# TensorE tile shapes in a two-layer graph attention kernel: transposes as quarter products with the identity, scores in sixteen 32x32 tiles

## The chip, the cores and the metric

The kernel runs on one core of a Trainium2 chip. The metric is the device time of one execution in microseconds (us); three runs of the kernel before gave 3501.76, 3508.07 and 3508.48, so a median of 3508.07. One execution more was recorded by the hardware profiler, and every duration below comes from that one.

## The reference

For each of 16 graphs x is 1024 nodes by 256 features, and adj says which pairs of nodes are joined. Two layers follow each other; all numbers are float32.

```python
# layer 0: multi-head attention without projections, then an MLP
h = maximum(layernorm(x), 0)
normed = layernorm(h) * gamma1 + beta1          # 8 heads of 32 features: queries = keys = values
scores = einsum('bhqd,bhkd->bhqk', qkv, qkv) / sqrt(32)
attn = softmax(where(adj > 0, scores, -inf))
h = h + einsum('bhqk,bhkd->bhqd', attn, qkv)
y = layernorm(h) * gamma2 + beta2
x = x + h + gelu(y @ W1 + b1) @ W2 + b2
# layer 1: one head of graph attention, 256 wide
f = maximum(layernorm(x), 0);  u = f @ W
logits = (u @ a_1).T + u @ a_2 + (u @ a_12) @ u.T
att = softmax(where(adj > 0, leaky_relu(logits, 0.2), -9e15))
x = x + elu(f @ W_1 + (att @ f) @ W_2)
```

## The kernel before, in words

**Tiles and stages.** `fast_path` holds the whole program; `general_path` is a fallback that a flag would start. Per graph, `attention` (line 931) walks 32 units: 2 halves of 512 queries, 2 groups of 4 heads, 8 blocks of 128 keys; 512 units in all. A unit has two steps on TensorE. `scores` (line 935, product on line 950) multiplies, for each of four heads j, a 32x128 piece of keys with a 32x512 piece of queries. The transposed features `kT` have head j on partitions 32j to 32j+31, so each product sits on 32 rows of the array and all 128 columns; the result fills 128 partitions of a PSUM bank of its own (`s`). VectorE adds the mask (line 971), ScalarE takes the exponential (line 974). `weigh` (line 982, product on line 987) runs one unit later: the weights, 128 keys by 512 queries, are multiplied with 128x32 values of each head, on all 128 rows and 32 columns of the array (`o`). After 8 key blocks `total` (line 896) sums the weights with ones, 128x32 again (`den`), and `finish` (line 914) transposes sums and outputs (`ptds`, `ptos`), divides, and adds to `h`. The sums come out 32 times over, and only every 32nd column of the transposed sums is read.

Between the units lies the rest of the previous graph, in pieces: `expand` and `contract` (the MLP, `ph` and `po`), `project`, `values`, `weights`, `attend` (layer 1: `puT`, `pg`, `lg`, `pf`, `pa`). All their products go through the helper `matmul` (line 565), which cuts the 128 stationary columns in four quarters of 32, so that they have the shape of `o`, 128 rows by 32 columns:

```python
    quarters = [True]

    def matmul(out, lhsT, rhs, start=True, stop=True):
        if not quarters[0]:
            nc.tensor.matmul(out, lhsT, rhs, start=start, stop=stop)
            return
        for c in range(0, P, HD):
            nc.tensor.matmul(out[c : c + HD], lhsT[:, c : c + HD], rhs, start=start, stop=stop)
```

When the attention of the last graph is over, `close_attention` (line 1042) sets the flag to False, and what is left of the last graph is multiplied without quarters.

**Transposes.** Blocks of 128x128 are transposed with TensorE's transpose against the identity, on the whole array: two `ptk` groups per half of a graph (`turn` in `prologue`, line 796, product on line 801), `pty` (`turn` in `rest`, line 1107, line 1117), `ptf` (`turn1`, line 1187, line 1193), four blocks each and four groups of each kind per graph; and in `finish` `ptds` and `ptos` (line 922), four blocks each, four times per graph; once in `setup` (line 672).

**Order.** Six generators (`stream_a` for the units, `stream_b` for the rest, `stream_p`, `stream_c`, `stream_m`, `stream_s`) each name a place in time, and the one with the lowest place goes on; every engine then keeps the order in which its instructions were written. Transposes wait in a list, `turns`, which `make_turns` (line 885) empties just before the scores of a unit. Waits between engines are semaphores put in from the tiles' uses. PSUM: two score tiles of two banks each, one bank for `o`, three for all else.

Of the kernel before, what the change touches and what calls it, by code (L numbers as in the profile page):

```python
# [9 lines left out]
F32 = mybir.dt.float32  # L10
# [6 lines left out]
P = 128  # L17
# [476 lines left out]
def fast_path(  # L494
# [28 lines left out]
    nc = tc.nc  # L523
# [34 lines left out]
    def ps_tile(shape, name, dtype=F32):  # L558
        return psm.tile(shape, dtype, tag="ps", name=name)
# [5 lines left out]
    def matmul(out, lhsT, rhs, start=True, stop=True):  # L565
# [3 lines left out]
        for c in range(0, P, HD):  # L569
            nc.tensor.matmul(out[c : c + HD], lhsT[:, c : c + HD], rhs, start=start, stop=stop)  # L570

# [21 lines left out]

    ident = const.tile([P, P], F32, name="ident")
    make_identity(nc, ident)
    ident8 = const.tile([P, P], FP8, name="ident8")
    nc.vector.tensor_copy(ident8, ident, saturate=False)  # L600
    ones = const.tile([P, HD], F32, name="ones")
# [58 lines left out]
    def setup():  # L660
        wl, wa, wT, wb = (lp1.tile([P, DC, D], F32, tag="e1", name=f"stage_{i}") for i in range(4))
        weights_to_load.extend([(wl, W), (wa, a_12)])
        for t, src in rows_to_load:
            nc.sync.dma_start(t, src)
        for t, src in weights_to_load:
            nc.scalar.dma_start(t, src.rearrange("(c p) n -> p c n", p=P))
        yield

        for oc in range(DC):
            pt = ps_tile([P, DC, P], f"p_wT_{oc}")  # L670
            for ic in range(DC):
                nc.tensor.transpose(pt[:, ic, :], wl[:, ic, oc * P : (oc + 1) * P], ident)
            nc.scalar.copy(wT[:, oc, :], pt.rearrange("p c q -> p (c q)"))
        clock[0] += 0.5
        yield

        def product(dst, lhs, rhs, n, name):

            for oc in range(DC):
                pp = ps_tile([P, n], f"p_{name}_{oc}")  # L680
                for kc in range(DC):
                    matmul(
                        pp,
                        lhs[:, kc, oc * P : (oc + 1) * P],
                        rhs[:, kc, :n],
                        start=(kc == 0),
                        stop=(kc == DC - 1),
                    )
                nc.scalar.copy(dst[:, oc, :], pp)

        product(wb, wa, wT, D, "wb")
        clock[0] += 1.7
        yield
        product(wm, wT, wb, D, "wm")
        product(w_a2.unsqueeze(2), wT, a2c.unsqueeze(2), 1, "w_a2")
        product(wo2[:, :, D : D + 1], wT, a1c.unsqueeze(2), 1, "w_a1")
        nc.gpsimd.memset(wo2[:, :, D + 1 : D + 2], 0.0)
        clock[0] += 2.0
        yield


        sq = lp1.tile([P, DC * D], F32, tag="e1", name="sq")
        few = smallp.tile([P, 2 * DC], F32, tag="few", bufs=1, name="few")
        wmf = wm.rearrange("p c n -> p (c n)")
        nc.vector.tensor_tensor(sq, wmf, wmf, op=ALU.mult)
        nc.vector.tensor_tensor(few[:, :DC], w_a2, w_a2, op=ALU.mult)
        nc.vector.tensor_tensor(few[:, DC:], wo2[:, :, D], wo2[:, :, D], op=ALU.mult)
        nc.vector.tensor_reduce(seen[:, 0:1], sq, axis=mybir.AxisListType.X, op=ALU.add)
        nc.vector.tensor_reduce(seen[:, 1:2], few, axis=mybir.AxisListType.X, op=ALU.add)
        yield  # L710
# [42 lines left out]
    def prologue(b, st):  # L753
# [42 lines left out]
        def turn(i):  # L796
            clock[0] += 0.5
            pt = ps_tile([P, NG, CW], f"ptk_{b}_{i}")
            for g in range(NG):
                for j in range(TPC):  # L800
                    nc.tensor.transpose(  # L801
                        pt[:, g, j * P : (j + 1) * P], va[:, i * TPC + j, g * P : (g + 1) * P], ident
                    )
            nc.scalar.copy(kT[:, :, i * CW : (i + 1) * CW], pt)

        steps = [
# [107 lines left out]
    def finish(b, qh, g, ds, os):  # L914
        h = hs[b]
        finished[b, qh] = finished.get((b, qh), 0) + 1
        clock[0] += 1.0
        pts = []
        for n, c in (("ds", ds), ("os", os)):
            pt = ps_tile([P, TPH, P], f"pt{n}_{b}_{g}_{qh}")  # L920
            for t in range(TPH):
                nc.tensor.transpose(pt[:, t, :], c[:, t * P : (t + 1) * P], ident)  # L922
            pts.append(pt.rearrange("p t (j d) -> p t j d", d=HD))
        rl = smallp.tile([P, TPH, GH], F32, tag="rl", name=f"rl_{b}_{g}_{qh}")
        nc.vector.reciprocal(rl, pts[0][:, :, :, 0])
        ot = tmpp.tile([P, TPH, GH, HD], F32, tag="w2", bufs=3, name=f"ot_{b}_{g}_{qh}")
        nc.vector.tensor_mul(ot, pts[1], rl.unsqueeze(3).to_broadcast([P, TPH, GH, HD]))
        ho = h[qh][:, :, g * P : (g + 1) * P]
        nc.gpsimd.tensor_add(ho, ho, ot.rearrange("p t j d -> p t (j d)"))

    def attention(b, st):
# [3 lines left out]
        def scores(qh, g, kt):  # L935
            qs = slice(qh * QW, (qh + 1) * QW)
            sc = [
                psc.tile([P, 2, QW], F32, tag=f"sc{i}", name=f"s_{b}_{g}_{qh}_{kt}_{i}") for i in range(2)
            ]

            by_pe = 2 if b == 0 else 0
            if by_pe:
                for j in range(by_pe):
                    matmul(
                        sc[j // 2][:, j % 2, :], ident8, st[qh][:, kt // 2, :, kt % 2], start=True, stop=False
                    )
                clock[0] += 0.45
            for j in range(GH):
                r = slice(j * HD, (j + 1) * HD)
                nc.tensor.matmul(  # L950
                    sc[j // 2][:, j % 2, :],
                    kT[r, g, kt * P : (kt + 1) * P],
                    kT[r, g, qs],
                    start=j >= by_pe,
                    stop=True,
                )
            mb = st[qh][:, kt // 2, :, kt % 2].unsqueeze(1).to_broadcast([P, 2, QW])
            es = []
            if b == 0 and kt % 2:

                odd = midp.tile([P, 2, 2, QW], F32, tag="mid", name=f"odd_{g}_{qh}_{kt}")
            for i in range(2):
                if b == 0 and kt % 2:
                    e = odd[:, i]
                elif kt == 0:
                    e = accp.tile([P, 2, QW], F32, tag=f"acc{i}", name=f"acc_{b}_{g}_{qh}_{i}")
                else:
                    e = ep.tile([P, 2, QW], F32, tag="e", name=f"e_{b}_{g}_{qh}_{kt}_{i}")
                masked = sc[i]
                if 2 * i >= by_pe:  # L970
                    nc.vector.tensor_tensor(e, masked, mb, op=ALU.add)  # L971
                    masked = e
                es.append(e)
                weights = lambda e=e, masked=masked: nc.scalar.activation(e, masked, AF.Exp, scale=SCALE)  # L974
                if i == 0:
                    weights()
            return es, weights
# [96 lines left out]
    def rest(b, st, tails):  # L1074
# [32 lines left out]
        def turn(c):  # L1107
            if st["y", c][1] is not None:
                run_deferred(st["y", c][1])
            y = st["y", c][0]  # L1110
            for i in range(TPC):
                defer(4.0 * i + 2.0, lambda t=c * TPC + i: add_residuals(t))
            yT[c] = tmpp.tile([P, DC, CW], F32, tag="yT", name=f"yT_{b}_{c}")
            pt = ps_tile([P, DC, CW], f"pty_{b}_{c}")
            for dc in range(DC):
                for i in range(TPC):
                    nc.tensor.transpose(  # L1117
                        pt[:, dc, i * P : (i + 1) * P], y[:, i, dc * P : (dc + 1) * P], ident
                    )
            for dc in range(DC):  # L1120
                nc.vector.tensor_scalar(
                    yT[c][:, dc, :],
                    pt[:, dc, :],
                    g2[:, dc : dc + 1],
                    be2[:, dc : dc + 1],
                    op0=ALU.mult,
                    op1=ALU.add,
                )
# [58 lines left out]
        def turn1(c):  # L1187
            run_deferred(ready1[c])
            fT = st["fT"]
            pt = ps_tile([P, DC, CW], f"ptf_{b}_{c}")  # L1190
            for i in range(TPC):
                for dc in range(DC):
                    nc.tensor.transpose(  # L1193
                        pt[:, dc, i * P : (i + 1) * P], ft[c][:, i, dc * P : (dc + 1) * P], ident
                    )
            nc.scalar.activation(fT[:, :, c * CW : (c + 1) * CW], pt, AF.Relu)

        def project(qh, oc, fT, uT):
# [343 lines left out]
```

## Time and profile before

| what | before |
|---|---|
| median of three runs | 3508.07 us (3501.76 to 3508.48) |
| the profiled execution | 3501.46 us |
| its span, first to last instruction | 3499.6 us, so 1.9 us lie around it |
| TensorE busy / VectorE / ScalarE / GpSimd | 98% / 79% / 53% / 40% |
| matmul records on TensorE | 46590, and as many weight loads |
| granted TensorE clock, mean | 0.998 |
| instruction fetch | 6.03 MB, 0.7% of the DMA engines' time |

A float32 product appears as two matmul records, each with a weight load of its own; a transpose as one. Four quarters of one product are four records that run side by side and start 6 to 7 ns apart; "a pass" below is one such set. A record lasts longer than the distance to the next pass[...]; so the cost of a block of instructions is read from the start of its first record to the start of the next block, and not from busy time. In the timeline view the columns are the start in us from the span's start, the length from the first start to the last end, the engine, the line, the operation, the tiles written and read, the part of the array used (rows*columns), the operand and the number of records. The releasers named in brackets are inferred by the profiler from semaphores.

### The profile page before, as it was taken

How to read it: one execution, taken by the hardware profiler on the slowest of the kernel's cores; microseconds unless marked ns; L12 is line 12 of the kernel's file. 1: busy time of each engine (PE TensorE's matmuls, PEld its weight loads, DVE VectorE, ACT ScalarE, POOL GpSimd, SP SyncE). 2: the span in 40 equal slices, each digit the busy share in tenths (PEclk: the TensorE clock that was granted, in tenths of full speed). 3: DMA queues.
4: the chain of work that ended last, by engine and by line, in shares of the span. 5: the costliest groups of instructions: out<-in, count | busy, mean ns of one | idle time of the engine just before them, and what ended most of it. 6: DMA issues, size and time to landing. Idle time of an engine off the chain costs nothing.

```text
span 3499.6 us, 107320 instructions
## 1 busy us (share of the span) xinstructions
PE 3445.0 (98%) x46590; PEld 1673.9 (48%) x46590; DVE 2758.3 (79%) x5193; ACT 1857.8 (53%) x2184; POOL 1412.8 (40%) x1708
## 2 busy tenths in 40 slices
PE   6999999999999999999999999999999999999998
PEld 2244444444444444444444444444444444444477
DVE  6878788787877878888787888878878777887754
ACT  4555555555555555555555555555555555555522
POOL 3444443434434344343444534344344443434220
PEclk9999999999999999999999999999999999999999
DMA  7798889999899998989989899998989989899720
GB/s 183 147 182 173 181 164 185 182 186 188 161 187 176 191 184 165 181 167 190 195 167 183 165 185 185 177 190 164 186 177 191 183 165 179 171 191 182 147 63 14
DMA packets 281860, 597.81 MB, mean 171 GB/s; under 512 B 94882, under 2 KB 130084, under 8 KB 281380
## 3 DMA queue, kind: packets, MB, share of 16 engines
q0 software_dynamic: 124416, 453.04, 70.1%
q1 hardware_dynamic: 154276, 134.41, 15.5%
q8 instruction: 368, 6.03, 0.7%
q10 hardware_dynamic: 2688, 3.41, 0.3%
q14 instruction: 112, 0.92, 0.1%
HBM read 104.21 MB, written 16.78 MB: 35 GB/s over the span
## 4 chain that ended last, share of the span: by engine, by line
PE 94%; DVE 3%; DMA 1%; issue 1%; ACT 0%; POOL 0%; ACTq 0%; SPq 0%; DVEq 0%; POOLq 0%
PE s L950 15%; PE o L987 13%; PE pa L570 12%; PE po L570 12%; PE ph L570 12%; PE lg L570 10%; PE pg L570 3%; PE pf L570 3%; PE puT L570 3%; PE den L901 2%; PE ptf L1193 1%; PE pty L1117 1%; PE ptk L801 1%; PE ptos L922 1%; PE pa L567 1%
## 5 line engine op out<-in xcount | busy, mean ns | idle before, releaser
L974 ACT ACTIVATE e<-e 128x1024 f32<-128x1024 f32 x852 | 896.0, 1057 | 964.3 <-DVE e L971 728.3
L1011 POOL DMA_DIRECT2D acc<-e x864 | 754.9, 890 | 1438.3 <-DMA acc<-e 637.3
L971 DVE TENSOR_TENSOR e<-s,mk 128x1024 f32<-128x1024 f32 x852 | 1002.6, 1217 | 181.2 <-PE s L950 155.4
L950 PE MATMUL s<-kT 32*128 32x512 f32 x4096 | 592.5, 643 | 3.5 <-DVE odd L971 2.7
L987 PE MATMUL o<-e,va 128*32 128x512 f32 x3456 | 461.8, 605 | 2.1 <-ACT e L974 2.1
L570 PE MATMUL pa<-gw,e 128*32 128x258 f32 x7648 | 453.0, 380 | 0.0
L570 PE MATMUL lg<-fT,uT 128*32 128x256 f32 x7680 | 447.3, 379 | 0.0
L570 PE MATMUL ph<-yT,w 128*32 128x256 f32 x7808 | 446.5, 379 | 0.0
L570 PE MATMUL po<-w,hid 128*32 128x256 f32 x7680 | 439.3, 379 | 0.0
L570 PEld LDWEIGHTS ph<-yT,w 128*32 128x32 f32 x7808 | 255.3, 110 | 211.8 <-issue 51.1
L570 PEld LDWEIGHTS po<-w,hid 128*32 128x32 f32 x7680 | 250.3, 110 | 208.8 <-issue 58.3
L570 PEld LDWEIGHTS pa<-gw,e 128*32 128x32 f32 x7648 | 248.4, 110 | 212.0 <-issue 56.5
L570 PEld LDWEIGHTS lg<-fT,uT 128*32 128x32 f32 x7680 | 249.6, 110 | 209.0 <-issue 43.4
L1241 DVE SCALAR_TENSOR_TENSOR e<-lg,gw,mk 128x256 f32<-128x256 f32 x512 | 223.2, 477 | 72.0 <-PE lg L570 61.5
L1247 ACT ACTIVATE e<-e,shift 128x512 f32<-128x512 f32 x256 | 183.1, 717 | 181.6 <-DVE e L1246 116.0
L1144 DVE TENSOR_TENSOR hid<-ph,b1c 128x512 f32<-128x512 f32 x256 | 175.8, 687 | 91.6 <-PE ph L570 80.1
L950 PEld LDWEIGHTS s<-kT 32*128 32x128 f32 x4096 | 162.7, 184 | 163.8 <-issue 112.0
L987 PEld LDWEIGHTS o<-e,va 128*32 128x32 f32 x3456 | 68.6, 108 | 330.3 <-issue 187.3
L974 ACT ACTIVATE acc<-acc 128x1024 f32<-128x1024 f32 x124 | 131.1, 1057 | 132.9 <-DVE acc L971 128.4
L1246 DVE SCALAR_TENSOR_TENSOR e<-e 128x512 f32<-128x512 f32 x256 | 193.1, 754 | 8.8
L971 DVE TENSOR_TENSOR acc<-s,mk 128x1024 f32<-128x1024 f32 x124 | 146.1, 1218 | 20.2 <-PE s L950 19.8
L793 POOL TENSOR_TENSOR nrm<-nrm,g 128x256 f32<-128x256 f32 x128 | 112.9, 882 | 63.8 <-DVE nrm L727 63.8
(145 smaller groups left out, 3820.9 us busy)
## 6 DMA issues: line engine op xcount, KB each, us to landing
acc<-e POOLq DMA_DIRECT2D x864, 512.0 KB, 6.1
adj<-in_adj_dram SPq DMA_DIRECT2D x248, 256.0 KB, 5.6
h<-in_x_dram SPq DMA_DIRECT2D x64, 256.0 KB, 6.1
xb<-in_x_dram SPq DMA_DIRECT2D x128, 128.0 KB, 4.3
out_dram<-z SPq DMA_DIRECT2D x128, 128.0 KB, 4.0
adj<-in_adj_dram SPq DMA_DIRECT2D x4, 512.0 KB, 6.8
mk<-mq SPq DMA_TRANSPOSE x128, 6.5
w<-in_L_gnn_W_dram ACTq DMA_DIRECT2D x2, 1024.0 KB
```

Of the source, the lines that this page charges most:

```text
L570: nc.tensor.matmul(out[c : c + HD], lhsT[:, c : c + HD], rhs, start=start, stop=stop)
L793: nc.gpsimd.tensor_mul(nrm, nrm, g1)
L901: nc.tensor.matmul(den[j * HD : (j + 1) * HD, :], ones, acc[j // 2][:, j % 2, :], start=acc is accs[0], stop=acc is accs[-1],)
L950: nc.tensor.matmul(sc[j // 2][:, j % 2, :], kT[r, g, kt * P : (kt + 1) * P], kT[r, g, qs], start=j >= by_pe, stop=True,)
L971: nc.vector.tensor_tensor(e, masked, mb, op=ALU.add)
L974: weights = lambda e=e, masked=masked: nc.scalar.activation(e, masked, AF.Exp, scale=SCALE)
L987: nc.tensor.matmul(o[j * HD : (j + 1) * HD, :], va[:, kt, (g * GH + j) * HD : (g * GH + j + 1) * HD], es[j // 2][:, j % 2, :], start=(kt = ...
L1011: nc.gpsimd.dma_start(sums[g, qh][i], e, accum_op=ALU.add)
L1144: nc.vector.tensor_tensor(hid[:, f0 : f0 + 2, :], ph, b1c[:, f0 : f0 + 2].unsqueeze(2).to_broadcast([P, 2, CW]), op=ALU.add,)
L1241: nc.vector.scalar_tensor_tensor(e[:, j, :], lg[:, j, :], gw[:, kt, D : D + 1], st[c // 2][:, kt // 2, qs, kt % 2], op0=ALU.add, op1=ALU.add,)
L1246: nc.vector.scalar_tensor_tensor(e, e, ALPHA, e, op0=ALU.mult, op1=ALU.max)
L1247: ready = defer(2.5, lambda: nc.scalar.activation(e, e, AF.Exp, bias=shift))
```

## The change

Every TensorE instruction of the main part gets stationary tiles of 32 columns. Transposes become plain products with the identity as the moving operand, in four quarters (while the flag is True). The transposed sums keep only the one column of each head that is read: the moving operand is then `each_head`, 128x4, every 32nd column of the identity. Each head's score product is cut in four along the keys, so that the sixteen products of a unit lie on 32x32 tiles of the array. The order of the blocks on each engine stays as it was; VectorE gets one small copy at the start.

```diff
+    def transpose(out, src, columns=None):
+
+        if not quarters[0]:
+            nc.tensor.transpose(out, src, ident)
+            return
+        for c in range(0, P, HD):
+            nc.tensor.matmul(
+                out[c : c + HD], src[:, c : c + HD], ident if columns is None else columns, start=True, stop=True
+            )
...
+    each_head = const.tile([P, GH], F32, name="each_head")
+    nc.vector.tensor_copy(each_head, ident[:, ::HD])
...
-                    nc.tensor.transpose(
-                        pt[:, g, j * P : (j + 1) * P], va[:, i * TPC + j, g * P : (g + 1) * P], ident
-                    )
+                    transpose(pt[:, g, j * P : (j + 1) * P], va[:, i * TPC + j, g * P : (g + 1) * P])
...
-        for n, c in (("ds", ds), ("os", os)):
-            pt = ps_tile([P, TPH, P], f"pt{n}_{b}_{g}_{qh}")
+        for n, c, rhs in (("ds", ds, each_head), ("os", os, ident)):
+            pt = ps_tile([P, TPH, rhs.shape[1]], f"pt{n}_{b}_{g}_{qh}")
             for t in range(TPH):
-                nc.tensor.transpose(pt[:, t, :], c[:, t * P : (t + 1) * P], ident)
-            pts.append(pt.rearrange("p t (j d) -> p t j d", d=HD))
+                transpose(pt[:, t, :], c[:, t * P : (t + 1) * P], rhs)
+            pts.append(pt)
...
-        nc.vector.reciprocal(rl, pts[0][:, :, :, 0])
+        nc.vector.reciprocal(rl, pts[0])
...
-                nc.tensor.matmul(
-                    sc[j // 2][:, j % 2, :],
-                    kT[r, g, kt * P : (kt + 1) * P],
-                    kT[r, g, qs],
-                    start=j >= by_pe,
-                    stop=True,
-                )
+                for c in range(0, P, HD):
+                    nc.tensor.matmul(
+                        sc[j // 2][c : c + HD, j % 2, :],
+                        kT[r, g, kt * P + c : kt * P + c + HD],
+                        kT[r, g, qs],
+                        start=j >= by_pe,
+                        stop=True,
+                    )
```

The transposes of `setup`, of `pty` and of `ptf` call the new helper in the same way.

More of the change, by code (lines that the diff above doesn't have):

```diff
@@ L671, in setup @@
             for ic in range(DC):
-                nc.tensor.transpose(pt[:, ic, :], wl[:, ic, oc * P : (oc + 1) * P], ident)
+                transpose(pt[:, ic, :], wl[:, ic, oc * P : (oc + 1) * P])
             nc.scalar.copy(wT[:, oc, :], pt.rearrange("p c q -> p (c q)"))
@@ L918, in finish @@
         pts = []
-        for n, c in (("ds", ds), ("os", os)):
-            pt = ps_tile([P, TPH, P], f"pt{n}_{b}_{g}_{qh}")
+        for n, c, rhs in (("ds", ds, each_head), ("os", os, ident)):
+            pt = ps_tile([P, TPH, rhs.shape[1]], f"pt{n}_{b}_{g}_{qh}")
             for t in range(TPH):
-                nc.tensor.transpose(pt[:, t, :], c[:, t * P : (t + 1) * P], ident)
-            pts.append(pt.rearrange("p t (j d) -> p t j d", d=HD))
+                transpose(pt[:, t, :], c[:, t * P : (t + 1) * P], rhs)
+            pts.append(pt)
         rl = smallp.tile([P, TPH, GH], F32, tag="rl", name=f"rl_{b}_{g}_{qh}")
-        nc.vector.reciprocal(rl, pts[0][:, :, :, 0])
+        nc.vector.reciprocal(rl, pts[0])
         ot = tmpp.tile([P, TPH, GH, HD], F32, tag="w2", bufs=3, name=f"ot_{b}_{g}_{qh}")
-        nc.vector.tensor_mul(ot, pts[1], rl.unsqueeze(3).to_broadcast([P, TPH, GH, HD]))
+        os_t = pts[1].rearrange("p t (j d) -> p t j d", d=HD)
+        nc.vector.tensor_mul(ot, os_t, rl.unsqueeze(3).to_broadcast([P, TPH, GH, HD]))
         ho = h[qh][:, :, g * P : (g + 1) * P]
@@ L1116, in turn @@
                 for i in range(TPC):
-                    nc.tensor.transpose(
-                        pt[:, dc, i * P : (i + 1) * P], y[:, i, dc * P : (dc + 1) * P], ident
-                    )
+                    transpose(pt[:, dc, i * P : (i + 1) * P], y[:, i, dc * P : (dc + 1) * P])
             for dc in range(DC):
@@ L1192, in turn1 @@
                 for dc in range(DC):
-                    nc.tensor.transpose(
-                        pt[:, dc, i * P : (i + 1) * P], ft[c][:, i, dc * P : (dc + 1) * P], ident
-                    )
+                    transpose(pt[:, dc, i * P : (i + 1) * P], ft[c][:, i, dc * P : (dc + 1) * P])
             nc.scalar.activation(fT[:, :, c * CW : (c + 1) * CW], pt, AF.Relu)
```

## The prediction

> **What bounds the kernel now.** First the page: which engine fills the span, and what the chain that ended last is made of.
>
> ```profile
> PE 3445.0 (98%) x46590; PEld 1673.9 (48%) x46590; DVE 2758.3 (79%) x5193; ACT 1857.8 (53%) x2184; POOL 1412.8 (40%) x1708
> ...
> PE 94%; DVE 3%; DMA 1%; issue 1%; ACT 0%; POOL 0%; ACTq 0%; SPq 0%; DVEq 0%; POOLq 0%
> ```
>
> Then TensorE's waits, to see whether that engine is held up by anything.
>
> ```profile
> PE ptk L801 <- POOL va L794: 22.2, 4, 19.3
> PE s L570 <- ACT acc L974: 8.1, 2, 5.5
> PE ptos L922 <- DVE e L1241: 3.4, 14, 0.2
> ```
>
> The largest three of twelve lines add to 33.7 us, all twelve to about 45 of 3499.6, most of it in the first graph. From there to the last graph TensorE never stands still, so only the length of its own stream counts. That is read from the timeline, start to start; first a stretch in the middle.
>
> ```profile
> 1696.95 1.91 PE L570 MATMUL ph<-yT,w 128*32 128x256 f32 x32
> 1698.68 1.91 PE L570 MATMUL po<-w,hid 128*32 128x256 f32 x32
> 1700.52 0.66 PE L1117 MATMUL pty<-ident,y 128*128 128x128 f32 x4
> 1701.11 1.14 PE L950 MATMUL s<-kT 32*128 32x512 f32 x8
> 1702.18 1.06 PE L987 MATMUL o<-acc,va 128*32 128x512 f32 x8
> 1703.06 3.64 PE L570 MATMUL po<-w,hid 128*32 128x256 f32 x64
> 1706.62 1.14 PE L950 MATMUL s<-kT 32*128 32x512 f32 x8
> 1707.70 1.06 PE L987 MATMUL o<-e,va 128*32 128x512 f32 x8
> 1708.58 1.04 PE L901 MATMUL den<-acc,ones 128*32 128x512 f32 x8
> 1709.44 1.91 PE L570 MATMUL po<-w,hid 128*32 128x256 f32 x32
> ```
>
> ph to po, the same shape on both sides: 1.73 us for 8 passes of 256 columns, 0.216 a pass. po to pty: the same 8 passes take 1.84, so 0.11 more at the change to 128*128. The 64 records of po, 16 passes, are worth 3.46, and the scores come 3.56 later: again 0.11. den, between equal shapes, takes 0.86 for two passes of 512 columns, 0.43 a pass. The scores take 1.07 for the same two passes, o 0.88. The records' own starts split this. After a change the next record starts 90 to 96 ns after the last one has streamed: an emptying of the array. A score's first record lasts 692 ns and its second 587, so 105 ns are the first load of weights that nothing covers; for o after the scores it is 617 against 592, 25 ns.
>
> The last graph, where nothing is cut in quarters, gives the counter-proof; after it the smallest products of the start.
>
> ```profile
> 3379.80 2.75 PE L567 MATMUL ph<-yT,w 128*128 128x256 f32 x12
> 3382.39 0.60 PE L1117 MATMUL pty<-ident,y 128*128 128x128 f32 x4
> 3382.83 1.46 PE L567 MATMUL po<-w,hid 128*128 128x256 f32 x6
> ...
> 73.00 0.43 PE L570 MATMUL p_w_a<-a1c,stage 128*32 128x1 f32 x32
> 73.36 0.66 PE L922 MATMUL ptds<-ident,ds 128*128 128x128 f32 x4
> ```
>
> Between products on the whole array four transposes take 0.44 us, 0.109 each, with no gap on either side (12 passes of ph are worth 2.59, and pty comes after 2.59). So it is the shape that costs, not transposing. In the middle the same four take 0.59: 0.44, 0.055 for a first load, and 0.093 to empty the array before the scores. That last change, 128*128 to 32*128, alters the rows alone, and still empties the array; the trace has 236 of it.
>
> [...] The trace has 6.7 ns between float32 tiles; I use that.
>
> **Transposes ahead of the scores.** A transpose is one record of 0.109; the product with the identity is a float32 product, two passes, and a pass of 128 columns is half of the 0.216: again 0.109. So four blocks cost 8 x 0.109 = 0.872 in place of 0.44. Saved are the change in front (0.113) and the first load (0.055); a change to the scores remains. Before, with both changes: 0.113 + 0.586 = 0.699. After: 0.872 + 0.113 = 0.985. That is +0.286 for each of 176 such groups (60 pty, 60 ptf, 56 ptk, counted in the trace): +50.3 us. Eight groups in the first graph and the setup are followed by 128*32; there the change behind goes too, and it is +0.15: +1.2. All of it is on TensorE and thus on the path. The last graph's six keep the old form: 0.
>
> **Transposes of sums and outputs.** Before: 0.113 + 1.022 for the pair. After, ptds has 4 moving columns: the nearest row is p_w_a with one column, 32 records whose starts span 0.26 us (0.43 less 0.17 for the last one), so 0.033 for a pass of four. 8 passes: 0.26. ptos as above 0.872, then the change 0.113: together 1.245, so +0.11 for 60 pairs: +6.6 us. Four more pairs lie elsewhere, about 0. From below ptds can't cost less than 0; from above 0.055 a pass, half of a 128-column pass: +11 us at most.
>
> **Scores.** Entry: 0.113 before; 0.113 after if the array empties between 128*32 and 32*32 too. First load: 32 columns as in o, 25 ns in place of 105: -0.080. Stream: two passes of 0.43, as before, since o shows that four column tiles stream beside each other at full rate and the scores now that four row tiles do. Tail: the array is empty when the last tile is, and the last of sixteen starts 15 x 6.7 = 100 ns after the first, in place of 3 x 6.7 = 20: +0.080. Exit: 0.09, then o's own first load, as now. Sum: 0 for each of 512. This is the choice that decides. Neither the entry nor the exit is shown for this pair of shapes; below, both vanish (rival one), above, the sixteen tiles cost more than I assume (rival two). [...]
>
> **What else changes.** VectorE's reciprocal reads 128x16 as before, and one copy of 128x4 is added ahead of the loop: 0. The order on VectorE, ScalarE, GpSimd and SyncE's queue is the same, and each has more slack if TensorE is slower. Instructions: 24 matmul records more in each unit (12288), 28 more in each of 311 groups of four blocks (185 single ones and two in each of 63 pairs; 8708): 67600 in place of 46590, so instruction fetch grows from 6.03 to 8.7 MB, from 0.7% of the DMA engines' time to 1.0%. The fetch is ahead now (issue is 1% of the chain); I take 0.
>
> **Sum.** 50.3 + 1.2 + 6.6 + 0 = +58 us on 3501.46, the profiled execution's own time: 3560. The median of the three runs lies 0.19% higher (3508.07), so 3566 would follow from there; I stay with 3560.
>
> **Rival one: no emptying between 32x32 and 128x32.** If only the column width counted, the main part would never change shape. Each unit then saves 0.113 at the entry and 0.025 in o, and the scores take 0.86 + 0.08 (o's first quarter needs the fourth row tile of its column, the thirteenth of sixteen, 12 x 6.7 ns) in place of 1.071: -0.269 x 512 = -138 us. With the +58 of the transposes: -80, so 3422, faster. It decides from the point where 58 of the 138, 0.113 a unit, are saved: a loss of just the entry would give no change. For it: nowhere in the trace do two shapes with 32 columns and different rows meet, so nothing excludes it. Against it: 128*128 to 32*128 differs in rows alone and empties, 236 times[...].
>
> **Rival two: sixteen tiles cost more than their start-to-start.** If the distance between tiles is twice the four-tile one, because 64 loads and products go through the sequencer in a unit that had 16, the tail is 0.20: +0.10 x 512 = +51, so 3611. Against it: eight loads and products in 32 ns are shown by p_w_a. For it: there it was one column.
>
> **How the numbers follow.** My forecast (the shape change still empties): 0.66, with its own range 3535 to 3595 ([...]part of rival two above). Rival one 0.24, its time 3422. Rival two 0.10. More than 2 in 10 would be left out without rival one, so the range reaches to it: 3412 to 3600. Some 0.2% is what a measurement of this kernel can tell from no change: 7 us. Faster 0.25 (rival one and a trace of better tails), same 0.02, slower 0.73.
>
> **What would show it.** In the changed profile four transposes of pty should take eight passes of 0.109, and ph or po before them should run into them without a gap. From the last pass of po to the first score record 0.31 should remain; from the first score to o 1.07. If instead score records start 0.196 after the last pass of a 256-column product, and o 0.94 after the first score, rival one is right. If score starts lie more than 7 ns apart, rival two. Waits of TensorE should stay near 45 us; if VectorE or ScalarE stands there with more, one of them has become late, and my 0 for them is wrong.

## The result, and the profile after

The changed kernel takes 3595.25 us in the median of four runs (3593.54 to 3596.1), the kernel before on the same chip 3508.28. The ratio is 1.0255, 95% interval 1.0243 to 1.0267: 87 us slower by the medians, 85 to 94 by the interval. The forecast was 3560 with a range of 3412 to 3600, slower with a chance of 0.73. The profiled execution has a span of 3594.3 us, 94.7 more than before.

TensorE still fills the span; the page's engine line shows 21108 matmul records more. In the chain that ended last TensorE has 90% in place of 94%, and the instruction fetch (q8) has grown from 6.03 MB to the 8.7 that the forecast had.

```profile
PE 3526.9 (98%) x67698; PEld 1883.7 (52%) x67698; DVE 2746.7 (76%) x5194; ACT 1862.4 (52%) x2184; POOL 1422.1 (40%) x1708
...
q8 instruction: 532, 8.72, 1.0%
...
PE 90%; DMA 4%; DVE 3%; issue 2%; ACT 1%; POOL 0%; ACTq 0%; SPq 0%; POOLq 0%; DVEq 0%
```

The timeline of TensorE in a stretch of the same kind as the one before (start, length, engine, line, operation, tiles, part of the array, operand, records):

```profile
1746.10 1.07 PE L578 MATMUL pty<-ident,y 128*32 128x128 f32 x32
1747.10 1.14 PE L964 MATMUL s<-kT 32*32 32x512 f32 x32
1748.17 1.08 PE L1001 MATMUL o<-acc,va 128*32 128x512 f32 x8
1749.06 3.65 PE L570 MATMUL po<-w,hid 128*32 128x256 f32 x64
1752.64 1.14 PE L964 MATMUL s<-kT 32*32 32x512 f32 x32
1753.71 1.08 PE L1001 MATMUL o<-e,va 128*32 128x512 f32 x8
1754.59 1.06 PE L912 MATMUL den<-acc,ones 128*32 128x512 f32 x8
1755.45 1.93 PE L570 MATMUL po<-w,hid 128*32 128x256 f32 x32
```

Three things are to be seen. The scores, now 32 records on 32*32, take 1.07 us from their start to o's, exactly as before on 32*128. The 64 records of po, 16 passes worth 3.46, are followed by the scores after 3.58: the 0.11 of a change of shape is still there, and in the single records some 0.016 has come on top. And pty takes 1.00 to the scores in place of 0.59. So the change of shape from 128*32 to 32*32 costs its 0.11 too, and the transposes are dearer. "Emptying" is a name for this gap: the first score starts 0.309 us after the last record of the product before it, 0.216 of it that record's own pass, so 0.093 lie between. The traces show how long the gap is, and not what the array does in it.

TensorE's waits, the longest of them (engine, tile and line that waited, who ended the wait, us in all, times, longest; "issue" means that nothing in the profile explains the wait):

```profile
PE ptk L578 <- POOL va L807: 21.1, 3, 19.1
PE ptos L578 <- DVE e L1251: 8.0, 14, 0.6
PE s L570 <- ACT acc L988: 7.3, 2, 4.8
PE ptf L578 <- issue: 5.4, 3, 2.7
PE s L570 <- issue: 2.8, 1, 2.8
...
PE po L570 <- issue: 2.1, 3, 1.0
```

ptos waits 8.0 us where it waited 3.4. Waits that end with "issue" stood nowhere in TensorE's list before; now there are six such lines, 11.8 us in all.

### The profile page after: what moved, and what is told of

It is laid out like the page before. It is cut to its first block, busy times and chain, and to the rows that moved or that the text cites. A ratio compares the mean times of both kernels' runs of the same rounds, so it can differ in the third digit from the quotient of the medians.

```text
span 3594.3 us, 149537 instructions
## 1 busy us (share of the span) xinstructions
PE 3526.9 (98%) x67698; PEld 1883.7 (52%) x67698; DVE 2746.7 (76%) x5194; ACT 1862.4 (52%) x2184; POOL 1422.1 (40%) x1708
## 4 chain that ended last, share of the span: by engine, by line
PE 90%; DMA 4%; DVE 3%; issue 2%; ACT 1%; POOL 0%; ACTq 0%; SPq 0%; POOLq 0%; DVEq 0%
PE s L964 15%; PE o L1001 13%; PE pa L570 12%; PE ph L570 11%; PE po L570 10%; PE lg L570 10%; DMA acc<-e 4%; PE pf L570 3%; PE pg L570 3%; PE puT L570 3%; PE ptos L578 2%; PE den L912 2%; PE ptk L578 1%; PE ptf L578 1%; PE pty L578 1%
## 5 line engine op out<-in xcount | busy, mean ns | idle before, releaser
L1025 POOL DMA_DIRECT2D acc<-e x864 | 763.0, 910 | 1498.1 <-DMA acc<-e 627.6
L964 PE MATMUL s<-kT 32*32 32x512 f32 x16384 | 597.2, 604 | 1.7 <-DVE odd L985 0.7
L1001 PE MATMUL o<-e,va 128*32 128x512 f32 x3456 | 469.6, 606 | 2.1 <-ACT e L988 2.1
L570 PEld LDWEIGHTS ph<-yT,w 128*32 128x32 f32 x7808 | 281.6, 110 | 185.7 <-issue 49.3
L570 PEld LDWEIGHTS po<-w,hid 128*32 128x32 f32 x7680 | 277.6, 110 | 187.1 <-issue 64.3
L570 PEld LDWEIGHTS pa<-gw,e 128*32 128x32 f32 x7648 | 272.4, 110 | 188.3 <-issue 54.2
L570 PEld LDWEIGHTS lg<-fT,uT 128*32 128x32 f32 x7680 | 273.4, 110 | 185.3 <-issue 41.8
L964 PEld LDWEIGHTS s<-kT 32*32 32x32 f32 x16384 | 122.6, 103 | 171.1 <-issue 133.6
```

The source lines that it names most:

```text
L964: nc.tensor.matmul(sc[j // 2][c : c + HD, j % 2, :], kT[r, g, kt * P + c : kt * P + c + HD], kT[r, g, qs], start=j >= by_pe, stop=True,)
L1001: nc.tensor.matmul(o[j * HD : (j + 1) * HD, :], va[:, kt, (g * GH + j) * HD : (g * GH + j + 1) * HD], es[j // 2][:, j % 2, :], start=(kt = ...
L1025: nc.gpsimd.dma_start(sums[g, qh][i], e, accum_op=ALU.add)
```

## The experiments

Times are medians; each run is compared with runs of the kernel before on the same chip. Their median was 3504.07 for the scores alone (sixteen and eight tiles), the transposes alone and the four columns alone, and 3503.58 for the outputs first, the two runs without accumulating DMAs and the last version. Traces are of one execution each.

**One half of the change at a time.** First the scores alone:

```diff
--- before
-                nc.tensor.matmul(sc[j // 2][:, j % 2, :], kT[r, g, kt * P : (kt + 1) * P], ...)
+                for c in range(0, P, HD):
+                    nc.tensor.matmul(sc[j // 2][c : c + HD, j % 2, :], kT[r, g, kt * P + c : kt * P + c + HD], ...)
```

> The kernel before with the scores in sixteen 32x32 tiles and nothing else changed. My theory (every change of tile shape empties the array): the first load falls by 0.080 us, the tail grows by 0.080, and the four quarters of the product o behind the scores start 37 ns apart in all instead of 20, which the changed kernel's trace shows: +0.016 x 512 = +8 us, and up to 6 us of late instruction fetch: 3516 to 3522. Rival (32x32 and 128x32 are one shape): -138 us, 3370. Rival (the scores are what makes the changed kernel slow): more than +40 us. From the first score to o 1.07 us by the first theory, 0.94 by the second.

Measured: 3515.05 us, ratio 1.0037 (1.0025 to 1.0049), so +9 to +17, 1 us under the expected window. From the first score to o it is 1.071 us in the median of 511 units. The rival "one shape for all" is out by over 140 us, and so is a large loss in the scores. The loss there is small: the four quarters of o's last pass start 36 ns apart in all where they started 20 before, and a unit without transposes, from its first score to the next unit's, is 16 ns longer in the median.

Then the transposes alone, with the scores put back to four products:

```diff
--- after
-                for c in range(0, P, HD):
-                    nc.tensor.matmul(sc[j // 2][c : c + HD, j % 2, :], kT[r, g, kt * P + c : kt * P + c + HD], ...)
+                nc.tensor.matmul(sc[j // 2][:, j % 2, :], kT[r, g, kt * P : (kt + 1) * P], ...)
```

> The changed kernel with the scores put back to four 32x128 products. My theory: the transposes carry the loss: +58 us as forecast, +5 for the wait of ptos for a PSUM buffer that the shorter ptds uncovers, a few us of late instruction fetch: +60 to +70, so 3568 to 3578. The quarters of o start 20 ns apart in all, as before. Rival (the scores carry a good part of the loss): under +40.

Measured: 3572.01, ratio 1.0195 (1.0182 to 1.0208), +64 to +73. This half carries most of the loss. A group of four takes 0.986 us to the scores, the forecast's 0.872 + 0.113; the quarters of o are 20 ns apart again. The pair of sums and outputs, in its timeline:

```profile
611.14 0.44 PE L578 MATMUL ptds<-each_head,ds 128*32 128x4 f32 x31
611.41 0.29 PE L578 MATMUL ptos<-ident,os 128*32 128x128 f32 x1
611.42 0.17 PE L578 MATMUL ptds<-each_head,ds 128*32 128x4 f32 x1
611.43 1.09 PE L578 MATMUL ptos<-ident,os 128*32 128x128 f32 x31
612.45 1.14 PE L963 MATMUL s<-kT 32*128 32x512 f32 x8
```

From the first ptds to the scores it is 1.31 us, where 1.245 had been forecast. The single records say why: the first 25 of ptds start 8 ns apart on average, a pass in 32 ns as forecast; from there on a record starts every 16.5 ns, so the quarters of ptos lie 50 ns apart in all. A first quarter of ptos even starts before the last one of ptds.

**Tiles of another size.** Each head's keys cut in two only:

```diff
--- before
+                for c in range(0, P, 2 * HD):
+                    nc.tensor.matmul(sc[j // 2][c : c + 2 * HD, j % 2, :], kT[r, g, kt * P + c : kt * P + c + 2 * HD], ...)
```

> The kernel before with each head's keys cut in two, so eight 32x64 tiles. My theory: first load of 64 columns 53 ns in place of 105, the last tile starts 7 x 6.7 = 47 ns after the first in place of 20: -0.025 x 512 = -13 us, so 3495; first score to o 1.045 us. [...] Rival (load and tail don't depend on the tile): 3508.

Measured: 3492.58, ratio 0.9966 (0.9953 to 0.9979): 12 us faster, by 7 to 16.

```profile
1704.91 1.11 PE L951 MATMUL s<-kT 32*64 32x512 f32 x16
1705.95 1.06 PE L988 MATMUL o<-e,va 128*32 128x512 f32 x8
```

1.04 from the scores to o, as expected: the first record lasts 638 ns against 587 for the second pass, a load of 51 in place of 105, and the last tile starts 47 ns after the first. o's quarters are 20 ns apart. The same sum that gives 0 for sixteen tiles gives the gain for eight.

**What pulls o's quarters apart.** The changed kernel with the order of the sixteen products turned:

```diff
--- after
-            for j in range(GH):
-                r = slice(j * HD, (j + 1) * HD)
-                for c in range(0, P, HD):
+            for c in range(0, P, HD):
+                for j in range(GH):
+                    r = slice(j * HD, (j + 1) * HD)
```

> The changed kernel with the sixteen score products in another order: all four heads of one column of tiles before the next column; nothing else. My theory: the array is emptied as a whole before o, and o's quarters start 37 ns apart in all[...]: from the first score to o 1.07 us, o's quarters 37 ns apart, span within 5 us of 3594. Rival (each quarter of o starts when its own column of tiles has ended): o's first quarter comes 80 ns earlier and its quarters lie some 80 ns apart.

Measured, in a single execution: 3592.35 us, span 3590.6; from the first score to o 1.071 in the median, the quarters of o's last pass 35 ns apart. So o starts after all sixteen tiles, not its first quarter after those of its own column (the 80 ns earlier of the rival), and the order of the tiles isn't what spreads the quarters. What does go with it is the number of instructions: 64 loads and products in the sixteen tiles, 32 in the eight. In two places, ptds with ptos and the scores with o, starts go from 7 or 8 ns apart to some 16.5, about 50 to 64 loads and products into a dense block. Not every such block shows it: the 32 records of p_w_a in the kernel before, 64 loads and products as well, start some 8 ns apart to the last, and in 77 of the changed kernel's 511 units the last of the sixteen tiles already start late (the sixteenth over 110 ns after the first). So the number of loads and products stays a candidate and not a shown cause.

**The four columns alone.** ptds as in the change, every other transpose as before:

```diff
--- before
+        for t in range(TPH):
+            matmul(ptds[:, t, :], ds[:, t * P : (t + 1) * P], each_head)
...
+            nc.tensor.transpose(ptos[:, t, :], os[:, t * P : (t + 1) * P], ident)
```

> The kernel before with ptds alone as quarter products with the four columns; ptos and all other transposes stay as they were. My theory: a pair takes 0.26 + 0.113 + 0.586 = 0.96 us in place of 0.113 + 1.022 = 1.135, -0.176 x 64 = -11 us, less some 3 us for 14 waits of ptos for a PSUM buffer: 3499 to 3501. Rival (the four-column products are bound by their loads at 0.055 a pass): 8 x 0.055 = 0.44, so 0 gain.

Measured: 3503.57, ratio 1.0001 (0.9989 to 1.0013), so none of the expected 3 to 5 us can be seen. The pair did become shorter on TensorE: 0.970 from ptds to the scores, with no change of shape ahead of it, against 0.113 + 1.022. But ptos waits 8.0 us for VectorE in place of 3.4, and this execution's trace has a stop of 2.5 us of the scores on VectorE, itself held up behind GpSimd and an accumulating DMA. Against the trace of the kernel before, the pairs are 10 us shorter in all, while 17 units without such a pair are together 14 us longer. Whether such stops belong to the edit or only happened in it isn't settled. What follows is that four-column passes are not bound by loads at 0.055 (0.970 - 0.113 - 0.586 leaves 0.27 for eight of them, not 0.44), and that a saving of 10 us on TensorE did not reach the end.

**The wait of ptos.** The changed kernel with the outputs first:

```diff
--- after
-        for n, c, rhs in (("ds", ds, each_head), ("os", os, ident)):
+        for n, c, rhs in (("os", os, ident), ("ds", ds, each_head)):
```

> The changed kernel with the transposes of the outputs (ptos) ahead of those of the sums (ptds), nothing else. My theory: in 14 of 64 pairs the second group waits for a PSUM buffer that VectorE still empties (8.0 us, against 3.4 in the kernel before), because ptds is over after 0.26 us; with the long group first the wait falls to 0, and the second group no longer starts its quarters 16 ns apart under a long group: -8 to -11 us against the changed kernel, so 3584 to 3587. Rival (the wait only moves to the first group of the pair): 3595.

Measured: 3585.64, ratio 1.0238 (1.0216 to 1.0260). The wait of ptos is gone from the list, the pair takes 1.258 in the median, and the time falls in the expected window; but the interval overlaps that of the changed kernel, so the trace shows the removal, and the time alone doesn't: against the changed kernel's trace the pairs lose 11 us in all, and the spans lie 9.5 apart. The trace shows one thing more. In 422 of 511 units the last of the sixteen score tiles start late (the sixteenth 114 ns after the first in the median), and o's quarters in the first pass are only 28 ns apart; yet o's last quarter starts 1.110 us after the first score, as in the changed kernel, where it was 1.091 before. So the slow starts sat in the scores here and in o there, and o's last quarter came at the same 1.110.

**Late instructions.** The changed kernel, and as a control the kernel before, without the accumulating DMAs, so without most of the softmax sums:

```diff
--- after, and the same to before
-            nc.gpsimd.dma_start(sums[g, qh][i], e, accum_op=ALU.add)
+            return
...
-        nc.scalar.copy(ds, den)
+        nc.scalar.activation(ds, den, AF.Identity, bias=large[:, 0:1])
```

> The changed kernel without the 864 accumulating DMAs of the attention weights, and with 1e6 added to their sums so that the quotients stay small: it leaves out most of the softmax sums. TensorE's stream is the same. My theory: the changed kernel's 11.8 us of issue waits on TensorE are instruction fetch that comes late behind these DMAs; without them they fall under 2 us, and the kernel takes 70 to 76 us more than the kernel before with the same cut, and about 3575. Rival[...]: they stay near 12 us, and the difference stays at 87.

> The control: the kernel before without the 864 accumulating DMAs, with 1e6 added to the sums. TensorE bounds it and hardly waits for these DMAs (1.9 us), so 3495 to 3505 by either theory, with no issue waits.

Measured: 3568.81 (3568.34 to 3570.43) and 3492.94, so 75.9 apart in place of 87. The changed kernel came out 6 us under the expected 3575, the control 2 us below the expected window and 11 us under the kernel before: it too loses some time to these DMAs. TensorE's longest waits without them:

```profile
PE ptk L578 <- POOL va L809: 20.9, 3, 18.8
PE ptos L578 <- DVE e L1253: 8.4, 14, 0.9
PE s L570 <- ACT acc L990: 7.7, 2, 4.9
PE o L1003 <- ACT e L990: 2.2, 2, 1.7
```

No line of the list ends with "issue" any more. The longest such stop in the changed kernel looks like this:

```profile
1115.76 3.21 PE L570 MATMUL po<-w,hid 128*32 128x256 f32 x56
1118.78 0.39 PE L578 MATMUL ptf<-ident,ft 128*32 128x128 f32 x5
1121.71 1.06 PE L578 MATMUL ptf<-ident,ft 128*32 128x128 f32 x27 [2.54 <-issue]
```

TensorE stops after 5 of 32 records of one group, in the middle of a product, where no tile can be missing. The packet of instructions fetched then took 3.49 us (median 0.96) and landed 1.5 us before the group went on; at the other stop of this length, at 3093, one landed 1.3 us before. After each of the two, from 1123.2 and from 3096.1 us, the granted clock is 0.50 for 3.4 us.

The other stops bear this out. The packets of queue q8, 368 before and 532 after, grow in step with TensorE's records, by a factor of 1.45 both. All eleven stops of the changed kernel that end with "issue" are over 1.27 to 1.62 us after such a packet has landed, and so are 15 of the 16 in the runs with the outputs first and with the order turned; all three runs have one in a ptf group near 1121 us. At a moment taken at random between 200 and 3400 us of the changed kernel the last packet lies 1.2 to 1.7 us back in 8% of the cases. So TensorE stood there for instructions that came late, and the rival, with 12 us left without the DMAs, falls. Ten of the eleven packets took no longer than 1.11 us, so in most stops it was not the transfer itself that was slow; why the packet came late beside these DMAs the traces don't show. The number of records alone doesn't set the stops: with the scores alone, 58878 records, there is none, with the transposes alone, 55410, there is one of 1.4 us, and without the DMAs none with 67698.

**A version faster than both.** Eight tiles and the four columns together:

```diff
--- before
+                for c in range(0, P, 2 * HD):
+                    nc.tensor.matmul(sc[j // 2][c : c + 2 * HD, j % 2, :], kT[r, g, kt * P + c : kt * P + c + 2 * HD], ...)
...
+            matmul(ptds[:, t, :], ds[:, t * P : (t + 1) * P], each_head)
```

> A version that should beat both: the kernel before with the scores in eight 32x64 tiles and the transposes of the sums as quarter products with four columns. The two edits alone gave -12 us and 0; the second saves TensorE 0.165 us in each of 64 pairs by its trace, -10.5 us, but uncovers 4.6 us of waits for a PSUM buffer: 3486 to 3493. Rival (the gain of the second edit is eaten in full by what comes after): 3492.6 as with the first alone.

Measured: 3492.23, ratio 0.9968 (0.9958 to 0.9978). Faster than the kernel before, but by the medians no more than with the eight tiles alone. The time lies at the upper end of the expected window and beside the rival's 3492.6, and the single executions reach from 3483.81 to 3511.59, so this run doesn't tell whether all of the second edit's gain is lost or only most of it.

## Why the prediction was right, and by how much it was short

The side was right and the time lies in the range, near its upper end; it is just past the 3535 to 3595 that the forecast had as its own. The forecast of +58 is 29 us short of the 87. Step by step:

- **The gap at the change of shape stays: right.** The first score still starts 0.309 us after the last record of the product before it in the median, and from the first score to o it is 1.071, before and after. Rival one, at 3422, fell with the same two numbers.
- **First load and tail of the scores cancel: right.** The first record lasts 612 ns against 587 (25 ns of load), the sixteenth tile starts 100 ns after the first with the scores alone and 103 in the changed kernel, in the medians. The eight tiles confirm both terms with other values.
- **Transposes ahead of the scores: right.** Eight passes of 0.109 with no gap in front, 0.986 in the run with the transposes alone, against a forecast of 0.985.
- **Sums and outputs: mis-sized.** 1.31 in place of 1.245, since beyond some 25 records a start takes 16.5 ns: 0.067 x 63 = +4 us.
- **"Exit: 0.09, then o's own first load, as now": mis-sized.** o's last quarter starts 19 ns later after the first score (1.110 in place of 1.091), and the quarters stay apart until the next change. Units without transposes are 17 ns longer in the median, so 0.017 x 512 = +9 us. Rival two had the size wrong, and mostly the place: in 434 of 511 units the sixteenth score tile starts within 110 ns of the first, close to the 100 that I had. But starts at more than twice the distance do occur, and what it named, 64 loads and products in a unit, is the candidate that is left.
- **"What else changes": failed in two points.** VectorE's order and work are the same, and I took 0; but the shorter ptds brings ptos ahead of the buffer that VectorE is still emptying: 8.0 - 3.4 = +5 us. And "the fetch is ahead now; I take 0" failed too: the trace lists 11.8 us of stops, and the accumulating DMAs make 11 us of difference between the two kernels by the medians. I went by an average, 1.0% of the DMA engines' time, for something that comes in a few places, and I gave it no upper bound. The sign I had named showed both: TensorE's waits add to 58 us where they should have stayed near 45.

58 + 4 + 9 + 5 = 76 without the fetch, and that is what the two kernels without the accumulating DMAs lie apart: 75.9 by the medians, 74.2 between their profiled executions. With these DMAs it is 11 us more by the medians, and 19 more between the two profiled executions, 94.7 apart; that of the kernel before, at 3501.46, is faster than all four of its timed runs (3501.76 to 3509.41). Where the 19 lie can be read by comparing each unit, from its first score to the next unit's, in both traces. After the first 150 us, and leaving out the pairs of sums and outputs, 27 of the 511 units differ by more than 0.06 us from the median of their kind; together they are 22 us longer. The first 150 us are 5 us shorter. Against the changed kernel without the DMAs it is 22 us as well, and between the two kernels without them nothing of the kind is left. Only some 8 of the 22 us stand in the list as stops that end with "issue"; the others are late starts under records that still run, waits for the DMAs themselves, and the two stretches of 3.4 us at a clock of 0.50, which can explain up to 3.4.

## What to carry to other kernels

When TensorE is the bound and never waits, count start to start per shape, and price every change of tile shape, of rows or of columns: here a gap of about 0.09 us, plus the first load, plus the distance between the first tile's start and the last one's. From 4 to 8 and 16 tiles the load fell from 105 to 51 and 25 ns and the distance grew from 20 to 47 and 100, so the middle number won here. A step that avoids a change is worth only that change: making four one-pass transposes two-pass products cost 0.43 us here to save 0.17. And cutting products in pieces multiplies instructions: with 21108 records more, stops for late instructions cost 11.8 us in eleven places, though the fetch's mean share was 1.0% of the DMA engines' time.

## What the runs showed of the hardware that I had not expected

- TensorE started the four-column records 8 ns apart for some 25 of them and later ones 16.5 ns apart; after the 64 loads and products of sixteen score tiles the four quarters of o were 36 ns apart in its last pass, after the 32 of eight tiles they were 20.
- An uneven start of the quarters persisted through the passes that followed in the same shape: in the changed kernel 37 ns in the first pass after o and 36 in the last before the next scores, 20 and 20 in the kernel before (medians of 105 such blocks). A unit paid 16 ns for it with the scores alone.
- TensorE lost 11.8 us to stops for which the profile shows no missing data when the program grew from 46590 to 67698 records beside 453 MB of accumulating DMAs, and none without those DMAs. Each of the eleven stops ended 1.27 to 1.62 us after a packet of instructions had landed.
